# Attention layer, then triangle layer: the second head pair's q and k loaded last in the passage and scored later, the last projections staged in small tiles, token scores and values issued in turn

## The chip, the cores and the metric

The kernel runs on one core of a Trainium2 chip. It is one program for four batch items, without a loop in the instructions: 58551 instructions in a fixed order on each engine. The metric is device time in microseconds. Three runs of the kernel before took 3699.86, 3704.49 and 3706.74 us, so the median is 3704.49 us. Engines are named as in the profile: PE (TensorE matmuls), PEld (its weight loads), DVE (VectorE), ACT (ScalarE), POOL (GpSimd), SP (SyncE, which here only issues DMAs).

## The reference, cut to what matters

Layer 0 is self-attention over 4096 tokens of 256 channels (32 for queries and keys, 128 for values). Layer 1 reads the result as a 64 x 64 grid and runs a triangle attention with 8 heads of 32 channels, an output product, layer norms and an MLP.

```python
def layer0(x):                       # b, 4096, 256
    f, g, v = x @ Wf + bf, x @ Wg + bg, x @ Wh + bh
    beta = softmax(einsum('bqd,bkd->bqk', g, f))
    return x + einsum('bqk,bkd->bqd', beta, v) @ Wo + bo

def layer1(x):                       # b, 64, 64, 256
    q, k, v1, v2 = x @ Wq, x @ Wk, x @ Wv1, x @ Wv2        # 8 heads of 32
    att = softmax(einsum('bilhd,bljhd->biljh', q, k) / sqrt(32), axis=2)
    out = einsum('biljh,bilhd,bljhd->bijhd', att, v1, v2)
    h = layer_norm(x + out @ Wo1)
    return layer_norm(relu(h @ W1 + b1) @ W2 + b2 + h)
```

## The kernel before

The four batch items b = 0 to 3 are handled one after the other. For each, `layer0` computes the token attention and writes the projections q, k, v1, v2 of its result to DRAM; then the triangle stage reads them back, for two heads (a "pair") at a time.

**Token attention.** There are 8 query blocks (`qb`) of 512 tokens and, for each, 8 groups (`k`) of four key tiles; a group is numbered `g`. `scores(g)` (line 526) issues four matmuls s (L531, operands in fp32r) into two PSUM tiles of tag "a" and then two exponentials on ACT (L541), each over half of the tile `e[g]`. `values(g)` (line 544) issues four matmuls o (L552, fp32, which the profile shows as eight passes) and one DVE addition to `esum` (L559). The loop issues `scores(g + 1)` and then `values(g)`, so that the exponentials of g + 1 run beside the values of g. Behind each group a "part" for the block before follows: the normalisation `norm` (L573 den, L575 reciprocal, L577), the output `y` (L598), and the projections (L613, L645). After the eighth group of a block DVE sums `esum` further (L562 to L566), and `norm` waits for that.

**The passage.** Lines 731 to 801 lead from token attention to the triangle stage: `norm(last)`, the last output and its projections, and the first pair's triangle scores (`score(0)` to `score(3)`, L857). Their results are staged in three `stage` tiles, which have the tag "R" of which there are three buffers, and stored on the ACT or SP queue. The products of the triangle stage use the same three buffers. In the passage of b > 0 the token-wise work of the item before (`rest.heads`, `rest.load`, `hidden`) is mixed in. `L.fetch_qk(1)` (line 790) issues the load of the second pair's q and k on the SP queue: four DMAs of 64 rows. Their two buffers are those of the first pair, so the load waits for `score(3)`.

**The triangle stage.** It has 32 steps of 8 rows i. The order of every engine's work is written out by hand in two lists of words, `ORDER0` for b = 0 (a period is four steps) and `ORDER` for b > 0 (a period is two steps). A word is an action, a piece and, behind the slash, by how many periods it lags. The words that matter here:

- `Rxm`: the product of attention and v2 (L959), on POOL for the last two or three m of a step and on DVE for the rest; `Axm`: its accumulation on PE (L969) into PSUM tiles of tag "a", of which there are two; `Txn`: ACT copies one of them out (L979).
- `Wx`, `tx`, `cx`, `Vx`: weights on ACT (L894), their transpose on PE (L911), POOL's copy (L919), the stationary operand (L938).
- `sp`: the triangle scores of the later pairs, one quarter of a pair at a time (L857, PSUM tag "a" too); `e0`, `e1`: their two exponentials (L867). The first `sp` of the stage scores quarter 0 of pair 1. It stands near the front of the first period that has work; pair 1 is first used in step 8.
- `h`, `ht`, `m`, `r`, `z`, `so`, `fo`, `fa`, `pp` and others: the token-wise work of the item before (b > 0), here L1028, L1128, L1161, L1181 on PE and small operations on the other engines. For b = 0, `P`, `C`, `g`, `a`, `b` prepare the inputs of the later items, from a tile `xin` that `ahead.load` fills, and `m`, `n`, `o`, `p` make late projections.

All engines take their instructions in the order in which they are issued. A DMA is issued on the SP queue in its turn, too; an instruction there that has to wait holds up those behind it.

Of the kernel before, what the change touches and what calls it, by code (L numbers as in the profile page):

```python
# [10 lines left out]
F32 = mybir.dt.float32  # L11
# [29 lines left out]


ORDER = """
    r0/1 A10/2 A11/2 m1/1 R14/2 R05/1 S1/1 R15/2 T10/2 sp/1 A14/2 A16/2 r1/1 e0/1 e1/1 A15/2 A05/1 T11/2
    R04/1 A04/1 z0/1 W1/1 R03/1 V1/1 fi/2 S0 z1/1 t1/1 so/1 R06/1 R00/1 c1/1 sa A03/1 R07/1 R02/1 A06/1
    A02/1 A00/1 rr/1 pp/1 W0 R01/1 A07/1 A01/1 fo/1 fa T01/1 R12/1 t0 T00/1 R17/1 h1/-1 R13/1 h0/-1 ht
    R16/1 hU A13/1 hT A12/1 A17/1 R11/1 c0 R10/1 m0 V0
""".split()


# [5 lines left out]
    A21/2 g1/2 S3/1 W1/1 A27/2 A23/2 A26/2 a1/2 V3/2 A24/2 P31/2 C21/2 R32/2 b1/2 m1/2 T20/2 c3/2 P30/2 C31/2  # L56
    t0/1 v2/2 n1/2 R25/2 A25/2 R33/2 sp0/1 T21/2 A32/2 C30/2 R34/2 R36/2 R30/2 A33/2 e00/1 u2/2 e01/1 o1/2 R31/2
    g2/2 P00/1 c0/1 R37/2 A34/2 A36/2 A30/2 A31/2 A37/2 V0/1 R35/2 C00/1 T30/2 t1/1 R00/1 p1/2 P01/1 a2/2 b2/2
    C01/1 A35/2 R03/1 T31/2 A00/1 R02/1 g0/1 a0/1 b0/1 R05/1 R07/1 A05/1 A03/1 v3/2 R06/1 u3/2 m0/1 S2/1 W2/1
    c1/1 v0/1 V1/1 R01/1 A02/1 n0/1 R04/1 A07/1 A01/1 A04/1 R12/1 P11/1 u0/1 P10/1 A06/1 T00/1 sp1/1 C11/1 T01/1  # L60
    R13/1 R15/1 R14/1 A13/1 e10/1 e11/1 t2/1 C10/1 R10/1 A12/1 R17/1 V2/1 A15/1 A14/1 A10/1 R16/1 R11/1 S0 R22/1
    W3/1 g3/2 c2/1 W0 A17/1 R27/1 A11/1 v1/1 R20/1 a3/2 b3/2 u1/1 o0/1 p0/1 S1 R21/1 T10/1 P20/1 t3/1 P21/1
    A16/1 T11/1 C20/1 A20/1 R23/1 A22/1 R24/1 R26/1
""".split()


# [1 line left out]
def attention_then_triangle_kernel(  # L68
# [408 lines left out]
                self.fetched = self.stored  # L477


    def layer0(b, F, safe, rest):  # L480
        yT, gT, fT = F.yT, F.gT, F.fT


# [39 lines left out]
        e, o_ps, esum, oT, ends, parts_of = {}, {}, {}, {}, {}, {}  # L523


        def scores(g):
            qb, k = divmod(g, 8)
            tt, n = divmod(k, 4)
            s_ps = [pa("s") for _ in range(2)]
            for r in range(4):  # L530
                nc.tensor.matmul(  # L531
                    s_ps[r // 2][:, r % 2, :], fT[tt][:, ts(r * 4 + n, P)], gT[qb // 4][:, ts(qb % 4, QB)],
                    start=True, stop=not safe,
                )
                if safe:
                    nc.tensor.matmul(
                        s_ps[r // 2][:, r % 2, :], ones_b[0:1, :], row[qb][0:1, :], start=False, stop=True
                    )
            e[g] = work.tile([P, 4, QB], F32, tag="k8", name="e")
            for j in range(2):  # L540
                nc.scalar.activation(e[g][:, 2 * j : 2 * j + 2, :], s_ps[j], AF.Exp)  # L541


        def values(g):
            qb, k = divmod(g, 8)
            tt, n = divmod(k, 4)
            if k == 0:
                o_ps[qb] = pc("o")
                esum[qb] = work.tile([P, 4, QB], F32, tag="Rp", name="esum")
            es = e.pop(g)  # L550
            for r in range(4):
                nc.tensor.matmul(  # L552
                    o_ps[qb], F.v[tt][:, r * 4 + n, :], es[:, r, :],
                    start=(k == 0 and r == 0), stop=(k == 7 and r == 3),
                )
            if k == 0:
                nc.vector.tensor_copy(esum[qb], es)
            else:
                nc.vector.tensor_tensor(esum[qb], esum[qb], es, ALU.add)  # L559
            if k == 7:  # L560
                halves = esum[qb]
                nc.vector.tensor_tensor(halves[:, 0:2], halves[:, 0:2], halves[:, 2:4], ALU.add)  # L562
                part = parts_of[qb] = work.tile([P, 2, QB], PART, tag="hid", name="part", bufs=1)
                nc.vector.tensor_tensor(part[:, 0], halves[:, 0], halves[:, 1], ALU.add)
                nc.vector.tensor_tensor(halves[:, 2], halves[:, 0], halves[:, 1], ALU.add)
                nc.vector.tensor_tensor(part[:, 1], halves[:, 2], part[:, 0].bitcast(F32), ALU.subtract)  # L566
# [132 lines left out]
            parts[6] = [lambda qb: proj(qb, "q", 1)]  # L699
            parts[7] = [lambda qb: proj(qb, "k", 1)]  # L700
        last = NQB - 1
        scores(0)
        for g in range(8 * NQB):
            qb, k = divmod(g, 8)
            if b == 0 and not safe:
                for load in later[3 * g : 3 * g + 3]:
                    load()
                if g == 6:
                    fold_bias()
                if g == 20:  # L710
                    add_b2()
            if safe and k == 0 and qb + 1 < NQB:
                mx, todo = pieces(qb + 1)
                for qc, t in todo:
                    max_piece(qc, t, mx)
                row[qb + 1] = max_row(mx)
            if g + 1 < 8 * NQB:
                scores(g + 1)
            values(g)

            if qb > 0 and not (qb == last and k >= 6 + late):
                for part in parts[k]:
                    part(qb - 1)
            if qb == last and k == 3:
                L.fetch_v1(0)
                L.fetch_v1(1)
            if qb == last and k == 5:
                if b > 0:
                    rest.load(NP * (b - 1))
                L.fetch_qk(0, True)  # L730
# [4 lines left out]
        old, t0 = b > 0, NP * (b - 1)  # L735
        stage = [work.tile([P, 4, QB], F32, tag="R", name="stage", bufs=3) for _ in range(3)]
        norm(last)
        if old:
            for n in range(2):
                rest.heads(t0, n, psum=pc)  # L740
# [45 lines left out]
        score(3)  # L786
        proj(last, "q", 1, None, stage[1][:, 3, :], nc.scalar)
        L.sums(0)
        proj(last, "k", 1, None, stage[2][:, 0, :], nc.scalar)
        L.fetch_qk(1)  # L790
        L.weights(0)
        hidden(1)
        L.turn(0)
        L.stationary(0)
        if not late:
            proj(last, "v2", 1, None, stage[2][:, 1, :], nc.scalar)
        if old:
            for n in range(2):
                rest.heads(t0 + 1, n)
            rest.load(t0 + 2)  # L800
        return L


# [3 lines left out]
    class Layer1:  # L807
# [10 lines left out]
        def fetch_qk(self, pair, first=False):  # L818
            io, rows = self.io, ts(pair, 64)
            qk = self.qk[pair] = [big.tile([P, 2048], F32, tag="qk", name=name, bufs=2) for name in ("q", "k")]  # L820
            n = 56 if first else 64
            for lh in range(2):
                half, lk = slice(64 * lh, 64 * lh + 64), min(n - 32 * lh, 32) * N
                nc.sync.dma_start(
                    out=qk[0][half, 0 : 32 * n], in_=io["q"][rows, lh, 0:n, :].rearrange("c i l -> c (i l)")
                )
                nc.sync.dma_start(out=qk[1][half, 0:lk], in_=io["k"][rows, 2048 * lh : 2048 * lh + lk])


        def fetch_v2(self, pair, part=None):  # L830
# [510 lines left out]

    def first_layer1(L, ahead, F):
        turned = {}
        ahead.load(0)

        def fetched(step):
            if 24 <= step < 31:
# [28 lines left out]
        for period in range(NSTEP // 4 + 3):  # L1376
            for word, late in words_of(ORDER0):
                i, last = period - late, int(word[-1])
                if word[0:2] == "sp":
                    if i >= 0:  # L1380
                        scores(2 * i + last)
                elif word[0] == "e":
                    if i >= 0:
                        take_scores(2 * i + int(word[1]), last)
                elif word[0] in "RATSWVtc":
                    step_word(word[0], 4 * i + int(word[1]), last)
                elif word[0] in "mnop":
                    if 0 <= i < 4:
                        own.word(word[0], 2 * i + last)
                elif 0 <= i < 4 and int(word[1]) < 2:  # L1390
                    front_word(word[0], 2 * i + int(word[1]), last)
                elif 4 <= i < 8:
                    front_word(word[0], 4 * i - 8 + int(word[1]), last)
# [3 lines left out]
    def next_layer1(b, L, rest, ahead, F):  # L1397
# [90 lines left out]
        for period in range(NP + 4):  # L1488
            for word, late in words_of(ORDER):
                i = period - late  # L1490
                if word[0] in "RATSWVtc":
                    step_word(word[0], 2 * i + int(word[1]), int(word[-1]))
                elif word == "sp":
                    scores(i)
                elif word in ("e0", "e1"):
                    take_scores(i, int(word[1]))
                else:
                    of_piece(word, i)
        assert not held
# [3 lines left out]
    def run(safe):  # L1503
        rest, ahead = Tokens(), Ahead()
        with tc.manual_schedule():
            F = front0(0)
            for b in range(NB):
                L = layer0(b, F, safe, rest)
                F = Front() if b + 1 < NB else None
                if F is None:  # L1510

                    rest.ios.append(L.io)
                if b == 0:
                    first_layer1(L, ahead, F)
                else:
                    next_layer1(b, L, rest, ahead, F)
                if F is not None:
                    rest.ios.append(L.io)
# [51 lines left out]
```

## Time and profile before

The profiled execution took 3700.29 us, of which 3698.4 us lie between its first and last instruction; the rest, 1.9 us, lies around it. The granted TensorE clock was 0.99 on average.

| engine | busy us | share of the span |
|---|---|---|
| PE | 3566.0 | 96% |
| DVE | 2682.0 | 73% |
| ACT | 1918.8 | 52% |
| POOL | 1761.5 | 48% |

The share of the chain that ended last belongs to PE with 80%, to POOL with 9%, to DMA with 3%, to DVE with 3% and to "issue" with 3%. Within the chain the largest lines are o (L552) with 23% and acc (L969) with 17%; s (L531) has 6%, and the transfer `k<-k` 2%.

How to read it: PE's idle time is small on the whole, but not evenly spread. A busy share of 96% says that most stages are bound by PE; where the chain leaves PE for a transfer or another engine, PE stood still. Such places are short and few, so views by time (the chain in order of time, the timeline, the windows) tell more here than sums over the span. A matmul's busy time includes the overlap with its neighbours; the distance between the starts of neighbours is what it costs. The profile shows an fp32 matmul as two passes.

### The profile page before, as it was taken

What the parts mean: (1) busy time and instruction counts of PE and PEld (TensorE: products, weight loads), DVE (VectorE), ACT (ScalarE), POOL (GpSimd) and SP (SyncE); (2) the same over time, 40 slices, a digit from 0 to 9 for tenths busy, and PEclk for the clock granted to TensorE, in tenths of its full rate; (3) what the DMA queues carried; (4) which work ended last, traced back from release to release, by engine and by line L of the source; (5) the groups of instructions that cost most, each with busy time, mean ns of one, the idle gap of its engine ahead of it and who ended that gap; (6) DMA issues with size and microseconds to landing.
All of it is one profiled execution on the core that took longest, in us unless ns stands there. A gap on an engine that the chain in (4) does not pass through costs nothing.

```text
span 3698.4 us, 58551 instructions
## 1 busy us (share of the span) xinstructions
PE 3566.0 (96%) x22602; PEld 1929.6 (52%) x22602; DVE 2682.0 (73%) x2142; ACT 1918.8 (52%) x4257; POOL 1761.5 (48%) x918
## 2 busy tenths in 40 slices
PE   9999899989999999998999999999899999999998
PEld 6555444444555555554455555554355555555477
DVE  4555599897555479999555449999755455999976
ACT  3333465554333367665433347676533335677654
POOL 5000199894000069999100019999700005999920
PEclk9999999999999999999999999999999999999999
DMA  8111566575111344425311153333511125431221
GB/s 149 47 46 46 146 166 161 146 168 147 51 51 52 104 103 94 97 48 100 71 52 51 49 143 89 75 91 65 117 42 50 52 73 136 98 90 49 68 65 56
DMA packets 461232, 324.01 MB, mean 88 GB/s; under 512 B 299984, under 2 KB 418512, under 8 KB 451600
## 3 DMA queue, kind: packets, MB, share of 16 engines
q1 hardware_dynamic: 411904, 293.21, 29.9%
q0 software_dynamic: 36160, 19.94, 4.8%
q10 hardware_dynamic: 12880, 7.01, 0.7%
q8 instruction: 181, 2.97, 0.3%
q14 instruction: 107, 0.88, 0.1%
HBM read 176.37 MB, written 143.65 MB: 87 GB/s over the span
## 4 chain that ended last, share of the span: by engine, by line
PE 80%; POOL 9%; DMA 3%; DVE 3%; issue 3%; ACT 1%; SPq 1%; ACTq 0%; POOLq 0%; DVEq 0%
PE o L552 23%; PE acc L969 17%; PE proj L613 8%; POOL Rp L959 7%; PE s L531 6%; PE mp L1161 5%; PE zp L1181 5%; PE sp L857 3%; PE hp L1028 2%; PE v1p L645 2%; PE y L598 2%; DMA k<-k 2%; DVE R L959 2%; PE att L911 1%; PE v1p L415 1%
## 5 line engine op out<-in xcount | busy, mean ns | idle before, releaser
L959 POOL TENSOR_TENSOR Rp<-attP,v 128x2048 f32<-128x2048 f32 x328 | 1491.2, 4573 | 430.3 <-ACT attP L919 349.5
L959 DVE TENSOR_TENSOR R<-att,v 128x2048 f32<-128x2048 f32 x696 | 1548.7, 2273 | 113.4 <-PE acc L969 71.2
L552 PE MATMUL o<-e,v 128*128 128x512 f32 x2048 | 919.8, 592 | 0.0
L559 DVE TENSOR_TENSOR esum<-esum,e 128x2048 f32<-128x2048 f32 x224 | 512.8, 2289 | 486.0 <-ACT e L541 482.9
L969 PE MATMUL acc<-R,wsel 128*32 128x512 f32 x5568 | 701.3, 601 | 14.9 <-ACT ao L979 7.8
L541 ACT ACTIVATE e<-s 128x1024 f32<-128x1024 f32 x512 | 496.6, 1025 | 312.5 <-PE s L531 152.3
L552 PEld LDWEIGHTS o<-e,v 128*128 128x128 f32 x2048 | 387.5, 189 | 391.8 <-issue 369.9
L1089 POOL TENSOR_SCALAR nt<-mv 128x4 f32<-128x4 f32 (+1 forms) x51 | 9.9, 194 | 1210.1 <-DVE mv L1045 1196.7
L531 PE MATMUL s<-gT,fT 128*128 128x512 f32 x1024 | 362.0, 474 | 8.7 <-ACT e L541 5.5
L969 PE MATMUL acc<-Rp,wsel 128*32 128x512 f32 x2624 | 347.5, 601 | 20.4 <-POOL Rp L959 19.5
L979 ACT COPY ao<-acc 128x1024 f32<-128x1024 f32 x256 | 254.6, 1020 | 177.5 <-PE acc L969 159.4
L969 PEld LDWEIGHTS acc<-R,wsel 128*32 128x32 f32 x5568 | 155.0, 110 | 355.1 <-issue 280.2
L894 ACT ACTIVATE es<-S,rd 128x64 f32<-128x64 f32 x1024 | 257.8, 336 | 15.9 <-DVE rd L886 14.4
L531 PEld LDWEIGHTS s<-gT,fT 128*128 128x128 f32 x1024 | 190.9, 189 | 134.5 <-issue 94.6
L1161 PE MATMUL mp<-hT,w 128*128 128x256 f32 x1024 | 249.5, 389 | 0.7 <-ACT hT L1133 0.7
L575 DVE RECIPROCAL rec<-den 128x512 f32<-128x512 f32 x32 | 107.4, 3358 | 193.4 <-PE den L573 193.4
L1181 PE MATMUL zp<-w,hid 128*128 128x256 f32 x1024 | 245.3, 385 | 0.8 <-ACT hid L1170 0.8
L1161 PEld LDWEIGHTS mp<-hT,w 128*128 128x128 f32 x1024 | 186.5, 190 | 101.4 <-ACT hid L1170 36.9
L1181 PEld LDWEIGHTS zp<-w,hid 128*128 128x128 f32 x1024 | 185.8, 190 | 65.0 <-issue 29.3
L625 ACT COPY st<-proj 128x512 f32<-128x512 f32 x98 | 57.5, 587 | 304.7 <-PE proj L613 169.8
L969 PEld LDWEIGHTS acc<-Rp,wsel 128*32 128x32 f32 x2624 | 80.7, 110 | 202.1 <-issue 125.7
L867 ACT ACTIVATE S<-sp 128x512 f32<-128x512 f32 x128 | 129.8, 1117 | 97.6 <-PE sp L857 74.1
(179 smaller groups left out, 3641.7 us busy)
## 6 DMA issues: line engine op xcount, KB each, us to landing
v<-v2d SPq DMA_DIRECT2D x44, 512.0 KB
v1c<-v1d SPq DMA_DIRECT2D x128, 128.0 KB
aT<-ao SPq DMA_DIRECT2D x1024, 16.0 KB
A<-aT SPq DMA_DIRECT2D x256, 64.0 KB
out_dram<-z SPq DMA_DIRECT2D x63, 256.0 KB
y<-yT SPq DMA_DIRECT2D x56, 256.0 KB
q<-st SPq DMA_DIRECT2D x56, 256.0 KB
k<-k SPq DMA_DIRECT2D x28, 512.0 KB
```

What stands on the lines that cost most here:

```text
L531: nc.tensor.matmul(s_ps[r // 2][:, r % 2, :], fT[tt][:, ts(r * 4 + n, P)], gT[qb // 4][:, ts(qb % 4, QB)], start=True, stop=not safe,)
L541: nc.scalar.activation(e[g][:, 2 * j : 2 * j + 2, :], s_ps[j], AF.Exp)
L552: nc.tensor.matmul(o_ps[qb], F.v[tt][:, r * 4 + n, :], es[:, r, :], start=(k == 0 and r == 0), stop=(k == 7 and r == 3),)
L559: nc.vector.tensor_tensor(esum[qb], esum[qb], es, ALU.add)
L613: nc.tensor.matmul(ps, w[:, cc, rows], y(qb, cc), start=(cc == 0), stop=(cc == 1))
L867: nc.scalar.activation(self.S[pair][:, :, l0 : l0 + 8].rearrange("p i l -> p l i"), sp[:, lh], AF.Copy if self.safe else AF.Exp,)
L894: nc.scalar.mul(e[:, i, :], rows[:, i, :], rec[:, i : i + 1])
L959: eng.tensor_tensor(R, src.unsqueeze(1).to_broadcast([P, D, N]), v2[h], ALU.mult)
L969: nc.tensor.matmul(acc[32 * c : 32 * c + 32, n % 2, :], w[:, n, c, 16 * h : 16 * h + 32], R[:, ts(c, 8), :].rearrange("p d j -> p (d j)"), ...
L979: nc.scalar.copy(self.ao[step][:, ts(np, 2)].rearrange("p k d j -> p k (d j)"), self.acc[step][np])
L1161: nc.tensor.matmul(self.mp[:, fc % 2, :], w1_sb[:, cc, ts(fc, P)], self.hT[tt][:, cc, :], start=(cc == 0), stop=(cc == 1),)
L1181: nc.tensor.matmul(zp[:, n, :], self.hid[tt][:, fc, ts(n, P)], w2_sb[:, fc, :], start=(fc == 0), stop=(fc == 3 and tt not in self.hT2),)
```

## The change

It has four pieces.

1. **Where pair 1's q and k are loaded.** `L.fetch_qk(1)` moves from the middle of the passage to its end, behind the load of the next token tile `rest.load(t0 + 2)`. For pair 1 the load of k is cut in two by columns, so that columns 0 to 511 of both halves come before the rest: two DMAs for q and four for k instead of two and two.
2. **Where pair 1 is first scored.** In both lists new words `sf`, `f0`, `f1` do the first quarter of pair 1; `sp`, `e0`, `e1` skip it. In `ORDER`, `sf` stands at the end of step 0, behind `T01`, `t0` and `T00`; in `ORDER0` it stands directly before `A00`.
3. **Where the last projections are staged.** k and (for b > 0) v2 of the last block use the small tiles of tag "st" instead of `stage[2]`. `stage[2]` then only holds the last block's y. For b = 0, `ahead.load(0)` is issued in the passage, behind `norm(last)`, instead of at the start of the triangle stage.
4. **Token scores and values.** `scores` becomes `score(g, r)`, one matmul; the exponential of a half follows its second matmul. `values(g)` now issues `score(g + 1, r)` before each of its four o matmuls, so the order on PE is s, o, s, o, s, o, s, o instead of s, s, s, s, o, o, o, o.

The arithmetic stays as it was.

```diff
@@ ORDER
-    R04/1 ... A01/1 fo/1 fa T01/1 R12/1 t0 T00/1 R17/1 h1/-1 R13/1 h0/-1 ht
-    R16/1 hU A13/1 hT A12/1 A17/1 R11/1 c0 R10/1 m0 V0
+    ... fo/1 fa T01/1 R12/1 t0 T00/1 sf/1 R17/1 h1/-1 R13/1 f0/1 h0/-1 ht f1/1 R16/1
+    hU A13/1 hT A12/1 A17/1 R11/1 c0 R10/1 m0 V0
@@ ORDER0
-    C01/1 A35/2 R03/1 T31/2 A00/1 R02/1 g0/1 a0/1 b0/1 R05/1 R07/1 ...
+    C01/1 A35/2 R03/1 T31/2 sf0/1 A00/1 R02/1 g0/1 f0/1 a0/1 b0/1 R05/1 f1/1 R07/1 ...
@@ layer0
-        def scores(g):
+        def score(g, r):
...
-            s_ps = [pa("s") for _ in range(2)]
-            for r in range(4):
+            if r == 0:
+                s_of[g] = [pa("s") for _ in range(2)]
+            s_ps = s_of[g]
...
+            if r % 2 == 1:
+                j = r // 2
                 nc.scalar.activation(e[g][:, 2 * j : 2 * j + 2, :], s_ps[j], AF.Exp)
...
             es = e.pop(g)
             for r in range(4):
+                if ahead:
+                    score(g + 1, r)
                 nc.tensor.matmul(
                     o_ps[qb], F.v[tt][:, r * 4 + n, :], es[:, r, :],
...
         norm(last)
+        if late:
+            ahead.load(0)
...
-        proj(last, "k", 1, None, stage[2][:, 0, :], nc.scalar)
-        L.fetch_qk(1)
+        proj(last, "k", 1, None, None, nc.scalar)
         L.weights(0)
...
-            proj(last, "v2", 1, None, stage[2][:, 1, :], nc.scalar)
+            proj(last, "v2", 1, None, None, nc.scalar)
         if old:
             for n in range(2):
                 rest.heads(t0 + 1, n)
             rest.load(t0 + 2)
+        L.fetch_qk(1)
@@ fetch_qk
             for lh in range(2):
-                half, lk = slice(64 * lh, 64 * lh + 64), min(n - 32 * lh, 32) * N
+                half = slice(64 * lh, 64 * lh + 64)
                 nc.sync.dma_start(out=qk[0][half, 0 : 32 * n], in_=...)
-                nc.sync.dma_start(out=qk[1][half, 0:lk], in_=io["k"][rows, 2048 * lh : 2048 * lh + lk])
+            for k0, k1 in ((0, QB), (QB, 2048)) if pair == 1 else ((0, 2048),):
+                for lh in range(2):
+                    half, lk = slice(64 * lh, 64 * lh + 64), min(k1, (n - 32 * lh) * N)
+                    nc.sync.dma_start(out=qk[1][half, k0:lk], in_=...)
@@ first_layer1
-        ahead.load(0)
@@ next_layer1 (first_layer1 alike)
-                elif word == "sp":
-                    scores(i)
-                elif word in ("e0", "e1"):
-                    take_scores(i, int(word[1]))
+                elif word in ("sp", "sf"):
+                    if (i == 0) == (word == "sf"):
+                        scores(i)
+                elif word in ("e0", "e1", "f0", "f1"):
+                    if (i == 0) == (word[0] == "f"):
+                        take_scores(i, int(word[1]))
```

More of the change, by code (lines that the diff above doesn't have):

```diff
@@ L43 @@
 ORDER = """
-    r0/1 A10/2 A11/2 m1/1 R14/2 R05/1 S1/1 R15/2 T10/2 sp/1 A14/2 A16/2 r1/1 e0/1 e1/1 A15/2 A05/1 T11/2
-    R04/1 A04/1 z0/1 W1/1 R03/1 V1/1 fi/2 S0 z1/1 t1/1 so/1 R06/1 R00/1 c1/1 sa A03/1 R07/1 R02/1 A06/1
-    A02/1 A00/1 rr/1 pp/1 W0 R01/1 A07/1 A01/1 fo/1 fa T01/1 R12/1 t0 T00/1 R17/1 h1/-1 R13/1 h0/-1 ht
-    R16/1 hU A13/1 hT A12/1 A17/1 R11/1 c0 R10/1 m0 V0
+    r0/1 A10/2 A11/2 m1/1 R14/2 R05/1 S1/1 R15/2 T10/2 sp/1 A14/2 A16/2 r1/1 e0/1 e1/1 A15/2 A05/1 T11/2 R04/1
+    A04/1 z0/1 W1/1 R03/1 V1/1 fi/2 S0 z1/1 t1/1 so/1 R06/1 R00/1 c1/1 sa A03/1 R07/1 R02/1 A06/1 A02/1 A00/1
+    rr/1 pp/1 W0 R01/1 A07/1 A01/1 fo/1 fa T01/1 R12/1 t0 T00/1 sf/1 R17/1 h1/-1 R13/1 f0/1 h0/-1 ht f1/1 R16/1
+    hU A13/1 hT A12/1 A17/1 R11/1 c0 R10/1 m0 V0
 """.split()
@@ L58 @@
     g2/2 P00/1 c0/1 R37/2 A34/2 A36/2 A30/2 A31/2 A37/2 V0/1 R35/2 C00/1 T30/2 t1/1 R00/1 p1/2 P01/1 a2/2 b2/2
[L59 to L63, printed above, removed]
+    C01/1 A35/2 R03/1 T31/2 sf0/1 A00/1 R02/1 g0/1 f0/1 a0/1 b0/1 R05/1 f1/1 R07/1 A05/1 A03/1 v3/2 R06/1 u3/2
+    m0/1 S2/1 W2/1 c1/1 v0/1 V1/1 R01/1 A02/1 n0/1 R04/1 A07/1 A01/1 A04/1 R12/1 P11/1 u0/1 P10/1 A06/1 T00/1
+    sp1/1 C11/1 T01/1 R13/1 R15/1 R14/1 A13/1 e10/1 e11/1 t2/1 C10/1 R10/1 A12/1 R17/1 V2/1 A15/1 A14/1 A10/1
+    R16/1 R11/1 S0 R22/1 W3/1 g3/2 c2/1 W0 A17/1 R27/1 A11/1 v1/1 R20/1 a3/2 b3/2 u1/1 o0/1 p0/1 S1 R21/1 T10/1
+    P20/1 t3/1 P21/1 A16/1 T11/1 C20/1 A20/1 R23/1 A22/1 R24/1 R26/1
 """.split()
@@ L477, in fetch, with layer0 @@
                 self.fetched = self.stored
-    def layer0(b, F, safe, rest):
+    def layer0(b, F, safe, rest, ahead):
         yT, gT, fT = F.yT, F.gT, F.fT
@@ L523, in layer0, with values @@
         e, o_ps, esum, oT, ends, parts_of = {}, {}, {}, {}, {}, {}
-        def scores(g):
+        s_of = {}
+        def score(g, r):
             qb, k = divmod(g, 8)
             tt, n = divmod(k, 4)
-            s_ps = [pa("s") for _ in range(2)]
-            for r in range(4):
+            if r == 0:
+                s_of[g] = [pa("s") for _ in range(2)]
+            s_ps = s_of[g]
+            nc.tensor.matmul(
+                s_ps[r // 2][:, r % 2, :], fT[tt][:, ts(r * 4 + n, P)], gT[qb // 4][:, ts(qb % 4, QB)],
+                start=True, stop=not safe,
+            )
+            if safe:
                 nc.tensor.matmul(
-                    s_ps[r // 2][:, r % 2, :], fT[tt][:, ts(r * 4 + n, P)], gT[qb // 4][:, ts(qb % 4, QB)],
-                    start=True, stop=not safe,
-                )
[L535 to L540, printed above, removed]
+                    s_ps[r // 2][:, r % 2, :], ones_b[0:1, :], row[qb][0:1, :], start=False, stop=True
+                )
+            if r == 0:
+                e[g] = work.tile([P, 4, QB], F32, tag="k8", name="e")
+            if r % 2 == 1:
+                j = r // 2
                 nc.scalar.activation(e[g][:, 2 * j : 2 * j + 2, :], s_ps[j], AF.Exp)
-        def values(g):
+            if r == 3:
+                s_of.pop(g)
+        def values(g, ahead):
             qb, k = divmod(g, 8)
@@ L701, in layer0 @@
         last = NQB - 1
-        scores(0)
+        for r in range(4):
+            score(0, r)
         for g in range(8 * NQB):
@@ L716, in layer0 @@
                 row[qb + 1] = max_row(mx)
-            if g + 1 < 8 * NQB:
-                scores(g + 1)
-            values(g)
+            values(g, g + 1 < 8 * NQB)
             if qb > 0 and not (qb == last and k >= 6 + late):
@@ L826, in fetch_qk @@
                 )
-                nc.sync.dma_start(out=qk[1][half, 0:lk], in_=io["k"][rows, 2048 * lh : 2048 * lh + lk])
+            for k0, k1 in ((0, QB), (QB, 2048)) if pair == 1 else ((0, 2048),):
+                for lh in range(2):
+                    half, lk = slice(64 * lh, 64 * lh + 64), min(k1, (n - 32 * lh) * N)
+                    nc.sync.dma_start(
+                        out=qk[1][half, k0:lk], in_=io["k"][rows, 2048 * lh + k0 : 2048 * lh + lk]
+                    )
         def fetch_v2(self, pair, part=None):
@@ L1379, in first_layer1 @@
                 if word[0:2] == "sp":
-                    if i >= 0:
+                    if 2 * i + last > 0:
                         scores(2 * i + last)
                 elif word[0] == "e":
-                    if i >= 0:
+                    if 2 * i + int(word[1]) > 0:
                         take_scores(2 * i + int(word[1]), last)
+                elif word[0:2] == "sf":
+                    if i == 0:
+                        scores(0)
+                elif word[0] == "f":
+                    if i == 0:
+                        take_scores(0, last)
                 elif word[0] in "RATSWVtc":
@@ L1507, in run @@
             for b in range(NB):
-                L = layer0(b, F, safe, rest)
+                L = layer0(b, F, safe, rest, ahead)
                 F = Front() if b + 1 < NB else None
```

## The prediction

> **What bounds the kernel.** I first read the chain of waits as a whole: 80% of it is PE, so a stage gains only if PE stands still in it. Then I asked for the chain in order of time. It leaves PE for long in the same place for every item: behind the last projections of the passage. For b = 3, the passage and then the triangle stage:
>
> ```profile
> 3076.61 3.65 PE proj L613 x8
> ...
> 3084.76 10.75 DMA k<-k
> 3095.51 0.14 issue
> 3095.65 2.03 PE sp L857 x62
> 3097.68 3.57 PE acc L969 x16
> 3101.25 2.21 PE zp L1181 x8
> ...
> 3106.06 5.29 PE acc L969 x48
> 3111.34 0.59 PE att L911 x4
> ...
> 3114.53 2.71 PE acc L969 x24
> ```
>
> Columns: start, duration, engine, target, line, count. PE cannot go on before pair 1's q and k have landed. The timeline of PE and DVE says how long each stood still (in brackets: idle before, and what ended it):
>
> ```profile
> 3090.76 0.38 PE L857 MATMUL sp<-q,k 32*64 32x64 f32 x2 [3.21 <-DMA k<-k]
> 3095.65 2.03 PE L857 MATMUL sp<-q,k 32*64 32x64 f32 x62 [4.50 <-DMA k<-k]
> ...
> 3096.21 2.29 DVE L959 TENSOR_TENSOR R<-att,v 128x2048 f32<-128x2048 f32 x1 [6.64 <-DMA v2d<-stage]
> ```
>
> PE idles 7.7 us; DVE waits until 3096.21 for its third buffer R, which is `stage[2]`, held by the v2 store. So two locks open at nearly the same moment, and the change must open both.
>
> The windows add the clock (columns: width, then busy of PE, PEld, DVE, ACT, POOL, then granted clock, DMA share, GB/s):
>
> ```profile
> 3084.00:3102.00 18.00, 10.29 (x99) 5.65 (x98) 9.28 (x10) 5.96 (x19) 11.27 (x3) 0.72 0.79 169
> 3102.00:3120.00 18.00, 18.00 (x134) 9.95 (x135) 14.49 (x7) 12.33 (x39) 13.84 (x11) 1.00 0.07 15
> ```
>
> The clock is 0.72 around the stall and 1.00 behind it. The chain prices this: 16 acc passes take 3.57 us, where 48 take 5.29 later (so 16 cost 1.76). The other passages show the same chain (k<-k of 10.83 us at 1310.54, for instance).
>
> **Pieces 1 to 3, b > 0, worked on b = 3.** *Before:* from the end of the heads at 3087.6 to the next accumulation of step 1 (A13) at 3114.5, 26.9 us. *After*, engine by engine, with the same durations:
>
> - POOL: its two products run 3084.3 to 3093.3 as now, the third follows directly, 4.5 us, to 3097.9. The `pp` polish, 2.0 us (3107.6 to 3109.8 before), ends at 3100.0.
> - DVE: two products and a sum to 3089.5, then, since `stage[2]` is free once the projections have read y (3085.4), R00 to 3091.8, statistics 1.2 to 3093.0, R02 to 3095.3, R01 (whose buffer A03 frees) to 3098.5.
> - PE: A05 waits for POOL's first product until 3088.9, so 1.3 us idle stay. Then A05 and A04 1.8, z 4.1, att 0.4, six accumulations 5.3, att 0.6: 3101.1. None waits; the nearest are A07, 0.8 us behind POOL, and A01, 1.1 us behind R01.
> - ACT: es(1) and the operand of step 1 no longer wait behind the exponentials and are ready by 3089. Behind z come the squares 1.9, copy, roots, es(2) 2.0 (3099.5), then from 3100.0 `fo` and `fa` 1.9, then T01 1.0: 3102.8.
> - `sf` needs a PSUM tile, and the oldest is the one that T01 frees. PE waits 1.7 us here, a **new wait** in front of heads (2.2), htp (0.4) and A13: sf 3102.85 to 3104.8, A13 at 3107.4.
>
> Gain: 3114.5 - 3107.4 = **7.1 us**. With the wait at `sf` gone it would be 8.8; that is the upper end.
>
> Queues. SP: the load of `rest.load(t0 + 2)` waits until 3087.4 for the heads, as now, but no longer behind the lane that the v2 store held (its second DMA went out at 3096.1). Its five issues take 2 us, then the six of q and k follow from about 3089.5 to 3093.3, then v1c. What `sf` needs is both halves of q and 512 columns of k, 1.25 MB. At the 169 to 182 GB/s of these windows that is 7 us plus 1 to 2 for the tile loads ahead: landed near 3098.5, 4 us before `sf`. All 2 MB land near 3103; v1c(2) behind them is needed at about 3109 by V0. Nothing waits, with 4 us to spare. The v2 store, which took from 3086.0 to 3096.1 beside these loads, is ahead of them now.
>
> [...] the change makes six of at most 512 KB out of four. The row: each of these issues takes 0.45 to 0.59 us on SP, so two more cost 1.2 us there, inside the 4 us. [...] by the row it is unchanged as long as `sf` waits for T01. I take the row.
>
> [...] By the idle row alone a passage would gain 7.7 - 1.3 - 1.7 = 4.7 us; with the slow passes (1.8 acc, 0.5 z, 0.1 sp) it is the 7.1 above. The window's 0.72 decides for the latter.
>
> **b = 0.** PE idles 0.9 and 4.5 us before the same scores. Here `sf` comes earlier, at 443.8 (the transposes of xin, 0.7, first; es(1); two more), and the load still starts at 432.25 when `score(3)` ends; its first 1.25 MB should be there near 441.5. But A05 needs the PSUM tile that `f1` frees, and `f1` stands behind `a0`, which needs `g0`: 449.2, where it ran at 451.5. DVE's second product still waits for the q store in `stage[1]` (445.6). PE and DVE both come out **2.4 us** ahead (ends: 0 and 4.2).
>
> **Piece 4, where it loses.** ACT now gets its second half only behind s, o, s, o, s, o, s. The rows that price it, last groups of b = 3:
>
> ```profile
> 3040.55 1.93 ACT L541 ACTIVATE e<-s 128x1024 f32<-128x1024 f32 x2
> ...
> 3042.51 2.29 DVE L559 TENSOR_TENSOR esum<-esum,e 128x2048 f32<-128x2048 f32 x1 [5.52 <-ACT e L541]
> ...
> 3048.17 0.50 PE L573 MATMUL den<-part,ones_f 128*128 128x512 f32 x1 [0.18 <-DVE part L566]
> ```
>
> DVE waits for ACT, PE's den for DVE: no slack for b > 0. The group's s starts at 3039.8. Now both exponentials end 2.7 us later. After: four s at 0.234 and three o at 0.858 make 3.5, plus 0.2 to ACT and 1.03: 4.7. So the den, and everything behind it, is **2.1 us late** for each b > 0. For b = 0 a projection stands between (den at 409.2, DVE done at 407.8), so 0.7.
>
> **Piece 4, inside the 256 groups.** PE's timeline for a group with a projection on each side:
>
> ```profile
> 2863.70 1.88 PE L613 MATMUL proj<-yT,wq 128*128 128x512 f32 x4
> 2865.01 1.50 PE L531 MATMUL s<-gT,fT 128*128 128x512 f32 x4
> 2866.35 3.60 PE L552 MATMUL o<-e,v 128*128 128x512 f32 x8
> 2869.78 0.59 PE L613 MATMUL proj<-yT,wk 128*128 128x512 f32 x1
> ```
>
> o: 3.43 / 8 = 0.429 a pass. The projection's four passes end at 2865.41, so four s take 0.94, 0.234 each, and the last s before o is as long as the others. PE is gapless, so there is no wait to hide; each s, o and its weight load remain. I take 0. [...] The high end is a price per change between fp32r and fp32: 6 more changes in a group, 1536 in all; the rows show under 3 ns (4.6 us). At each start of token attention the first o need not wait for the second scores: 0.2 us (b > 0), 0.8 (b = 0).
>
> **Sum.** b > 0: 3 x (7.1 - 2.1 + 0.2) = 15.6. b = 0: 2.4 - 0.7 + 0.8 = 2.5. Together 18 us: the span 3698.4 becomes 3680, the profiled execution 3700.3 becomes 3682. That execution lay 4.2 us under the median of the three runs, which it shares as an offset, so I predict 3704.5 - 18 = **3686.5 us**.
>
> **Rivals.**
>
> - *R0, as above*: 3680 to 3694. Chance 0.62.
> - *R1, s becomes faster between o's*: [...] Against: the last s, in front of o, is not shorter than the rest now. 0.1.
> - *R2, the gain is swallowed*: `sf` waits for q and k after all, or the den wait (2.1 us idle, in two parts) brings half the clock again. If `sf` had to wait another 4 us in each item, 3704.5 - 18 + 16 = 3702; half of that, 3694. For: between 1755 and 1760 PE is idle for 2.9 of 5 us, and the window 1760.3 to 1763.8 has a clock of 0.51. Against: 4 us to spare. 0.18.
> - *R3, slower*: alternating fp32r and fp32 costs PE at each change. Break-even at 18 / 1536 = 12 ns; at 25 ns, +38 - 18 = +20, 3725. Against: the start of o behind s and of s behind a projection shows nothing of it. 0.05.
> - *R4, the change doesn't do what it says*: o(g, 0) waits for both exponentials. In groups without a part the second ends 4.7 us after the group's start and o(g, 0) stands at 4.6, so 0.2 to 0.4 us in 39 groups: 8 to 16 us, some 3699. Against: the first two `sp` matmuls ran when only their half of q and k had landed, so waits are by region. 0.05.
>
> 0.2% is 7.4 us, about what a measurement can tell from no change: between 3697.1 and 3711.9 is "the same". Faster: R0, R1, half of R2, some of R4: 0.85. Same: the rest of R2 and R4: 0.1. Slower 0.05. Range **3670 to 3698**.
>
> **What would show it.** No idle of PE before `sp` by `k<-k` in any passage; clock 1.00 there; the third R right behind the sum; a wait of 1 to 2 us at `sf` ended by ACT's `ao`; PE's idle before den grown from 0.2 to 2.3 us for b > 0. Starts of s and o 0.234 and 0.429 apart, a group of 4.37. Wrong if the distance of s moves by more than 5 ns, if `sf` is released by a DMA, or if half clock follows the den.

## The result, and the profile after

The changed kernel takes **3686.80 us** (median of 6 runs, 3684.63 to 3689.25), the kernel before 3703.47 us in the 6 runs beside it. The ratio is 0.9954, with an interval of 0.9942 to 0.9967: 16.7 us less. In the profiled executions the span went from 3698.4 to 3683.3 us, 15.1 less, and the mean granted clock from 0.990 to 0.994.

First the chain of waits in order of time, the passage of b = 3 (start, duration, engine, target, line, count):

```profile
3073.95 4.55 POOL Rp L974
3078.51 0.04 issue
3078.55 1.92 PE acc L984 x16
...
3089.58 1.02 ACT z L1120 x2
3090.61 0.91 ACT h L1120 x2
3091.52 0.91 ACT ao L994
3092.43 0.04 issue
3092.47 2.08 PE sp L872 x58
3094.55 1.72 PE hp L1043 x4
...
3099.03 2.71 PE acc L984 x24
```

The 10.75 us of `k<-k` are gone from the chain. In their place stand ACT's two operations `fo` and `fa` (z, h) and the copy `ao` that frees a PSUM tile; then comes `sf`, in the place of the former `sp`. The timeline of PE and DVE at the same place (in brackets: idle before, and what ended it):

```profile
3078.31 0.68 DVE L899 TENSOR_REDUCE dens<-S 128x8 f32<-128x512 f32 x1
3079.02 0.20 DVE L901 RECIPROCAL rd<-dens 128x8 f32<-128x8 f32 x1
3079.14 2.25 DVE L974 TENSOR_TENSOR R<-att,v 128x2048 f32<-128x2048 f32 x1
...
3092.47 2.08 PE L872 MATMUL sp<-q,k 32*64 32x64 f32 x64 [1.59 <-ACT ao L994]
```

DVE's third R follows the sum without a wait; it waited 6.64 us before. PE waits 1.59 us for `ao`, and no longer for a transfer. The windows (width, busy of PE, PEld, DVE, ACT and POOL, clock, DMA share, GB/s):

```profile
3074.00:3092.00 18.00, 15.54 (x107) 8.31 (x105) 16.48 (x13) 11.00 (x41) 17.43 (x11) 1.00 0.80 175
3092.00:3110.00 18.00, 17.53 (x208) 11.28 (x212) 12.59 (x8) 9.57 (x19) 13.63 (x5) 0.91 0.53 123
```

The first shows full clock where 0.72 stood before. The second has 0.91: behind the wait at `sf`, the clock is 0.50 for 3.4 us, from 3094.8 to 3098.2.

Where the time went is best seen by cutting each item at two points: from its first s to its last den (token attention), from there to the first accumulation of step 1 (passage), and from there to its last accumulation (triangle stage). All numbers are differences of starts in the trace, in us; of three numbers, they are b = 1, 2, 3.

| kernel | token attention, b > 0 | passage, b > 0 | triangle, b > 0 | b = 0: all three |
|---|---|---|---|---|
| before | 390.7 391.9 391.9 | 66.0 66.2 66.3 | 428.7 428.6 424.6 | 368.4 55.3 415.1 |
| changed | 392.2 392.5 392.5 | 59.5 59.5 61.1 | 428.5 428.6 424.6 | 369.1 55.1 414.1 |
| changed, again | 392.1 392.4 392.3 | 60.6 59.4 59.4 | 428.3 428.4 424.5 | 370.4 55.6 417.6 |
| group 63 plain | 390.2 390.4 390.5 | 61.0 61.1 61.1 | 428.4 428.5 424.6 | 368.4 55.3 414.7 |
| turns only | 392.2 392.4 392.4 | 65.3 65.3 63.3 | 429.0 428.9 424.6 | 368.6 55.5 415.3 |
| `sf` behind heads | 392.1 392.4 392.4 | 58.7 58.7 58.7 | 428.9 428.9 425.2 | 368.1 53.8 416.8 |
| score later only | 390.4 391.8 391.8 | 65.6 64.1 63.7 | 428.5 428.6 424.6 | 370.0 60.4 416.3 |
| no turns | 390.4 391.9 391.8 | 60.9 60.4 59.4 | 428.3 428.3 424.5 | 369.2 55.3 414.3 |
| load early | 392.2 392.4 392.4 | 60.6 59.4 61.1 | 428.3 428.4 424.5 | 370.4 55.8 417.7 |
| `stage[2]` | 392.2 392.4 392.4 | 62.1 60.6 59.4 | 428.3 428.3 424.5 | 368.8 55.1 414.1 |
| k whole | 392.3 392.5 392.4 | 60.6 59.5 59.5 | 428.5 428.6 424.6 | 369.1 55.6 415.8 |
| three edits | 390.1 390.3 390.4 | 57.6 57.5 57.5 | 428.9 429.0 425.1 | 368.6 53.4 416.8 |
| three edits, again | 390.1 390.3 390.3 | 57.6 57.6 57.5 | 428.9 429.0 425.1 | 367.5 52.0 412.5 |
| three edits, no turns | 390.9 391.8 391.8 | 57.6 57.5 57.5 | 429.0 429.2 425.3 | 370.2 53.3 416.0 |

Two readings. For b > 0 the changed kernel gains 18.4 us in the passages (6.5 + 6.7 + 5.2) and gives back 2.7 in token attention. And b = 0 moves by up to 5 us between two executions of one kernel (its triangle stage took 414.1 and 417.6), so small effects have to be read at b > 0. There two executions of one kernel agree to 0.2 us in each stage, except for steps of 1.1 to 1.7 us in the passage. These steps are half clock, taken up last.

### The profile page after: what moved, and what is told of

It is laid out like the page before. It is cut to its first block, busy times and chain, and to the rows that moved or that the text cites. A ratio compares the mean times of both kernels' runs of the same rounds, so it can differ in the third digit from the quotient of the medians.

```text
span 3683.3 us, 58564 instructions
## 1 busy us (share of the span) xinstructions
PE 3562.0 (97%) x22602; PEld 1930.0 (52%) x22602; DVE 2682.3 (73%) x2142; ACT 1963.3 (53%) x4257; POOL 1763.0 (48%) x918
## 4 chain that ended last, share of the span: by engine, by line
PE 70%; POOL 7%; issue 3%; DMA 3%; DVE 3%; ACT 2%; SPq 0%; ACTq 0%; POOLq 0%; DVEq 0%
PE acc L984 18%; PE o L561 18%; POOL Rp L974 6%; PE proj L622 6%; PE zp L1196 5%; PE mp L1176 5%; PE s L534 5%; PE hp L1043 3%; PE sp L872 3%; PE v1p L654 2%; DVE R L974 1%; PE y L607 1%; PE att L926 1%; PE hp L1048 1%; PE htp L1143 1%
## 5 line engine op out<-in xcount | busy, mean ns | idle before, releaser
L974 POOL TENSOR_TENSOR Rp<-attP,v 128x2048 f32<-128x2048 f32 x328 | 1491.8, 4576 | 420.0 <-ACT attP L934 370.2
L561 PE MATMUL o<-e,v 128*128 128x512 f32 x2048 | 1043.4, 592 | 0.0
L546 ACT ACTIVATE e<-s 128x1024 f32<-128x1024 f32 x512 | 524.0, 1025 | 581.5 <-PE s L534 481.9
L534 PE MATMUL s<-gT,fT 128*128 128x512 f32 x1024 | 785.5, 769 | 8.9 <-ACT e L546 5.1
L1185 ACT ACTIVATE hid<-mp,b_sb 128x256 f32<-128x256 f32 x256 | 105.6, 471 | 117.5 <-PE mp L1176 117.5
```

The costliest lines, as they stand in the source:

```text
L534: nc.tensor.matmul(s_ps[r // 2][:, r % 2, :], fT[tt][:, ts(r * 4 + n, P)], gT[qb // 4][:, ts(qb % 4, QB)], start=True, stop=not safe,)
L561: nc.tensor.matmul(o_ps[qb], F.v[tt][:, r * 4 + n, :], es[:, r, :], start=(k == 0 and r == 0), stop=(k == 7 and r == 3),)
L974: eng.tensor_tensor(R, src.unsqueeze(1).to_broadcast([P, D, N]), v2[h], ALU.mult)
```

## The experiments

**1. Group 63 without turns.** All else as in the changed kernel.

```diff
-                if ahead:
+                if ahead and g + 1 < 8 * NQB - 1:
                     score(g + 1, r)
...
+            if g + 1 == 8 * NQB - 1:
+                for r in range(4):
+                    score(g + 1, r)
             values(g, g + 1 < 8 * NQB)
```

> The changed kernel, but the scores of the last group of each item (g = 63) are issued before the values of group 62, as before the change; all other groups stay in turns. Theory: PE's wait before den (1.23 + 0.77 us for b > 0, 0.52 for b = 0) is only the late second exponential of group 63, so it falls back to 0.2 and 0, and with it the slow output of b = 0 (3.50 us for y, where it took 1.96): 3 x 2.1 + 0.7 + 1.5 = 8 us less than the changed kernel, about 3679. Rival: the lateness is made up behind the den in any case (the passage waits for transfers), or PE's order inside the groups causes it: within 2 us of the changed kernel, about 3687.

Measured: 3680.96 us, ratio 0.9944 (0.9930 to 0.9957). PE's timeline at den for b = 1, changed kernel:

```profile
1274.55 0.47 PE L582 MATMUL den<-part,ones_f 128*128 128x512 f32 x1 [1.23 <-DVE part L573]
1275.79 0.50 PE L582 MATMUL den<-part,ones_f 128*128 128x512 f32 x1 [0.77 <-DVE part L575]
```

and with group 63 plain:

```profile
1272.98 0.50 PE L582 MATMUL den<-part,ones_f 128*128 128x512 f32 x1 [0.18 <-DVE part L575]
```

The two waits of 1.23 and 0.77 us shrink to the 0.18 of the kernel before; token attention falls from 392.2 to 390.2 in b = 1 and by 2.1 and 2.0 in the others. So the late den costs 2.0 to 2.1 us per item. The passages took 61.0 to 61.1 us, and in this execution all three had half clock behind `sf`; in the changed kernel a passage with it took 61.1 us (b = 3), and the two without it 59.5. Against the expectation, y of b = 0 stayed slow, 3.06 us.

**2. Turns alone.** Piece 4 on the kernel before.

> The kernel before with piece 4 alone (token scores and values in turn); loads, staging and the words for pair 1 as before. Theory: per item b > 0 it loses 2.1 us at den and gains 0.5 in the groups and 0 to 0.9 at the start; b = 0 loses 0.7 and perhaps 1.5 by the clock: together 3 to 5 us slower than the kernel before, about 3707, with half clock behind the transfer of k as before. Rival: the turns bring part of the gain of the change, so that it is 3 us or more faster than before.

Measured: 3701.84 us, ratio 1.0001 (0.9993 to 1.0009), so not the loss that was expected. The den is late (token attention +1.5, +0.5, +0.5 against before), but the passage takes 0.7, 0.9 and 3.0 us less. The wait at `sp` says why. Before, b = 1:

```profile
1316.51 0.38 PE L857 MATMUL sp<-q,k 32*64 32x64 f32 x2 [3.17 <-DMA k<-k]
1321.50 2.03 PE L857 MATMUL sp<-q,k 32*64 32x64 f32 x62 [4.62 <-DMA k<-k]
```

With turns alone:

```profile
1320.86 0.41 PE L870 MATMUL sp<-q,k 32*64 32x64 f32 x2 [4.19 <-DMA k<-k]
1323.19 2.04 PE L870 MATMUL sp<-q,k 32*64 32x64 f32 x62 [1.92 <-DMA k<-k]
```

The y of b = 1 was 3.4 us late in this run (1282.05 against 1278.61), and these scores are 1.7 us late: PE waited 6.1 us here instead of 7.8. A lateness ahead of such a wait is in part absorbed by it. In the changed kernel this cover is gone, which is why the 2.1 us count there (experiment 1). The passages of b = 1 and 2 also hold half clock behind the den, 1.2 us each, and that of b = 3 does not.

**3. `sf` behind the heads.** The changed kernel with `sf`, `f0` and `f1` moved back in `ORDER`.

```diff
-    ... T00/1 sf/1 R17/1 h1/-1 R13/1 f0/1 h0/-1 ht f1/1 R16/1 hU A13/1 hT A12/1
+    ... T00/1 R17/1 h1/-1 R13/1 h0/-1 ht sf/1 R16/1 hU A13/1 hT f0/1 f1/1 A12/1
```

> The changed kernel, with sf moved behind h1, h0 and ht in the list for b > 0, and f0, f1 behind hT. Theory: the wait of 1.6 us before sf (ended by ACT's ao) is for the PSUM tile that T01 frees; behind 2.6 us of other PE work the tile is free, so 1.6 us go per item b > 0, and the half clock of 3.4 us behind it in b = 3 (1.6 us more): 5 to 6.5 us less than the changed kernel, about 3681. Rival: sf waits for q and k, or A13 then waits in its place for the second tile that T00 frees: within 1.5 us of the changed kernel.

Measured: 3683.98 us, ratio 0.9949 (0.9935 to 0.9963); the interval overlaps that of the changed kernel. The passages took 58.7 us, although in this execution all three had half clock behind the den (1.2 us each, see the last section). The wait at `sf` therefore costs 1.9 us: 59.4, the best passage of the changed kernel, less 57.5, which is 58.7 less 1.2. The triangle stage gives some of it back: here and in experiment 8 it takes 0.3 to 0.6 us more than in the changed kernel (428.9, 428.9 and 425.2). In the version that combines this with experiment 1, PE's timeline for b = 3 reads:

```profile
3081.12 0.66 PE L929 MATMUL att<-ident,es 128*128 128x128 f32 x4
3081.61 1.07 PE L1046 MATMUL hp<-wo,A 128*128 128x256 f32 x4
...
3083.82 0.60 PE L1146 MATMUL htp<-ident,h 128*128 128x128 f32 x4
3084.35 1.99 PE L875 MATMUL sp<-q,k 32*64 32x64 f32 x64
3086.27 1.92 PE L987 MATMUL acc<-R,wsel 128*32 128x512 f32 x16
```

No line has a bracket: the heads (hp) and htp need no PSUM tile of tag "a", and while they run ACT frees the one that `sf` wants.

**4. The later score alone.** The kernel before with the words `sf`, `f0`, `f1` only: the load early and whole, `stage[2]`, no turns, `ahead.load(0)` where it was.

> The kernel before with piece 2 alone: pair 1 scored at sf, but q and k fetched where they were, k in two DMAs, the last k and v2 staged in stage[2], scores and values not in turns. Theory of two locks: PE is let go, but DVE's third product still waits until the v2 store has landed (the 6.6 us of before), so A02 and A01 wait for DVE; per item b > 0 some 2 to 3 us of the 7 are gained, in all 6 to 10 us less than before, about 3695. Rival: only PE's wait for k counted, and the staging and the order of loads do nothing: 3 x 7 + 2 = 23 us less than before, about 3680.

Measured: 3701.11 us, ratio 0.9996 (0.9987 to 1.0004). This is less than was expected. The passages of b > 0 gain 0.4, 2.1 and 2.6 us, and that of b = 0 loses 5.1, of which 1.4 by a y at half clock (3.31 us instead of 1.96). The timelines of DVE and PE for b = 3, then of PE for b = 0:

```profile
3101.55 2.29 DVE L973 TENSOR_TENSOR R<-att,v 128x2048 f32<-128x2048 f32 x1 [6.52 <-DMA v2d<-stage]
...
3107.16 3.24 PE L983 MATMUL acc<-R,wsel 128*32 128x512 f32 x16 [4.51 <-DVE R L973]
...
450.61 1.08 PE L345 MATMUL tp<-ident,xin 128*128 128x128 f32 x4 [7.64 <-DMA xin<-in_x_dram]
```

With the first lock open (PE no longer waits for k), the second one holds: DVE waits for `stage[2]`, and PE for DVE's R. The v2 store was issued at 3091.5, and DVE was released at 3101.5: 10 us. For b = 0 a third lock appears that the transfer of q and k had covered: the load of `xin`, issued behind them at 438.4. It is the reason for `ahead.load(0)` in the passage; the changed kernel without that one piece was not run.

**5. Which piece opens the second lock.** The changed kernel with the load of pair 1 in its old place ("load early"), and with the last k and v2 in `stage[2]` again.

```diff
-        proj(last, "k", 1, None, None, nc.scalar)
+        proj(last, "k", 1, None, stage[2][:, 0, :], nc.scalar)
...
-            proj(last, "v2", 1, None, None, nc.scalar)
+            proj(last, "v2", 1, None, stage[2][:, 1, :], nc.scalar)
```

> The changed kernel with pair 1's q and k loaded in the old place (directly behind proj k, ahead of the next token tile), the rest of the change kept. Theory (the load can stand anywhere that leaves it 4 us of slack; what counts is that sf is late and the staging small): the q and k land earlier, the token tile 1 to 3 us later but still in time, within 1.5 us of the changed kernel, 3685 to 3688 us. Rival (the 2 MB in front of the token tile delay the heads or the hidden layer, or DVE's y and xc tiles): 2 to 5 us slower in each passage, 3692 to 3700.

> The changed kernel with the last k and v2 staged in stage[2] again, load late. Theory (the third buffer R was locked by the v2 store for 10 us only because q and k were loading beside it; with the load behind, the store is over by the time that DVE wants the buffer, 1 to 3 us later than in the changed kernel at most): 0 to 1 us for each of three items, 3687 to 3690 us. Rival (the small tiles are what opens the lock): DVE's third R 4 us late, A01 and A02 wait 3 to 4 us, and three items lose 3 us each: 3695 to 3697.

Measured: 3684.14 us (ratio 0.9955, 0.9942 to 0.9969) and 3683.92 us (0.9955, 0.9941 to 0.9968), with the kernel before at 3700.89 us beside them. Both ratios are that of the changed kernel. Their best passages, 59.4, are also its best. DVE's timeline with `stage[2]`, b = 3:

```profile
3081.07 0.67 DVE L899 TENSOR_REDUCE dens<-S 128x8 f32<-128x512 f32 x1
3081.78 0.20 DVE L901 RECIPROCAL rd<-dens 128x8 f32<-128x8 f32 x1
3081.90 2.28 DVE L974 TENSOR_TENSOR R<-att,v 128x2048 f32<-128x2048 f32 x1
```

The third R has no bracket: the v2 store, issued at 3078.5, had released the buffer after at most 3.4 us. With q and k loading beside it, it took 10 (experiment 4). So **either** of the two pieces is enough, the store taken from the shared buffer or the load taken from beside the store. With neither (experiment 4) the passages of b > 0 gain 5.1 us in all instead of 18.4. That version also lacks the turns and the split of k, but experiments 6 and 7 take these out one at a time, and the passages of b > 0 stay as short but for half clock. What the score's later place is worth with both pieces kept and `sp` in its old place was not run.

**6. k whole.** The changed kernel with two DMAs for pair 1's k instead of four.

> The changed kernel with k of pair 1 loaded whole (two DMAs of 512 KB) instead of in two parts. Theory (sf waits for T01's PSUM tile, not for the transfer: all 2 MB land about when sf starts): 0 to 1 us per item, sf's wait still ended by ACT's ao: 0 to 3 us above the changed kernel. Rival (the first 512 columns land in time only because they are split off): sf waits 3 to 5 us for k in each of three items, 9 to 15 us slower.

Measured: 3691.09 us (ratio 0.9973, 0.9962 to 0.9984), beside the changed kernel again:

> The changed kernel once more, on the chip of the three runs beside it, so that differences of 2 us can be read: 3686 us, 16 to 18 below the kernel before.

That took 3688.80 us (0.9968, 0.9955 to 0.9980). The intervals overlap. PE's timeline with k whole, b = 3:

```profile
3095.69 2.08 PE L872 MATMUL sp<-q,k 32*64 32x64 f32 x64 [1.61 <-ACT ao L994]
```

`sf` still waits for `ao` and not for k: the split gains nothing that these runs can show.

**7. No turns.** Piece 4 undone in all groups.

> The changed kernel with all scores(g + 1) issued before values(g), as before the change: piece 4 undone in all 256 groups. Theory (the turns gain little in the groups, about 8 ns in each of 256 = 2 us, and lose 2.1 us at each den plus the half clock behind it): like the run with group 63 alone undone, 3681, plus 0 to 2.5: 3681 to 3684 us, so faster than the changed kernel by 3 to 6 us. Groups of 4.355 us against 4.348. Rival (the turns hide something at the start of token attention or give PE more): 3687 or slower.

Measured: 3681.85 us, ratio 0.9951 (0.9938 to 0.9965), 19.0 us below the kernel before where the changed kernel was 16.7 below: the sign as expected, but the two intervals overlap. The table is clearer. Against the changed kernel, token attention of b > 0 is 1.8, 0.6 and 0.7 us shorter without turns. Against group 63 plain it is 0.2, 1.5 and 1.3 us longer. So the turns gain up to 1.5 us in an item and lose 2.1.

The traces show where the gain lies. The start of b = 3, first in the kernel before, then with the turns of the changed kernel:

```profile
2656.30 0.73 PE L531 MATMUL s<-gT,fT 128*128 128x512 f32 x2
...
2659.93 3.60 PE L552 MATMUL o<-e,v 128*128 128x512 f32 x8
```

```profile
2645.36 0.73 PE L534 MATMUL s<-gT,fT 128*128 128x512 f32 x2
2646.40 1.95 ACT L546 ACTIVATE e<-s 128x1024 f32<-128x1024 f32 x2
2647.83 1.02 PE L561 MATMUL o<-e,v 128*128 128x512 f32 x2
```

From the first s to the first o it is 3.63 us before and 2.47 in turns, where three fewer s stand between them (0.70 us), so the start gains 0.46 us. From there to the first o of group 62 both orders issue the same matmuls: 380.8 us without turns and 379.8 with them in b = 2 and 3, but 379.6 and 379.8 in b = 1 (no turns and changed kernel). So the groups gain 1.0 us in two items and lose 0.2 in one. Why is open.

**8. All three.** The changed kernel with experiments 1 and 3, and in `ORDER0` `f1` directly behind `f0`, so that A05 of b = 0 gets its PSUM tile earlier.

```diff
-    ... g0/1 f0/1 a0/1 b0/1 R05/1 f1/1 R07/1 A05/1 ...
+    ... g0/1 f0/1 f1/1 a0/1 b0/1 R05/1 R07/1 A05/1 ...
```

> The changed kernel with three edits: group 63's scores all before values(62), sf behind the heads with f0 and f1 behind hT (b > 0), and for b = 0 f1 directly behind f0. Theory (the den's wait and the wait at sf each cost what the first two runs of them alone showed, and the two add): 5.8 us from the den, 2.8 from sf, about 1 from f1 in b = 0 (A05 waited 1.73 us for f1's tile): 3686.8 - 9.6 = about 3677 us, range 3674 to 3680. PE idle before den 0.2 us in all items, no wait at sf, A05 of b = 0 without its 1.7 us. Rival (each edit only moves the lateness to the next wait, and half clock returns in each passage at another place): 3680 to 3682, no better than the den edit alone.

> The version with group 63 plain, sf behind the heads and f1 directly behind f0, once more: 11 to 13 us below the changed kernel on the same chip.

Measured: 3672.50 us, ratio 0.9923 (0.9910 to 0.9937), below the expected range, and again, on another chip, **3667.35 us**, 0.9909 (0.9893 to 0.9924), beside 3688.80 of the changed kernel there, nearly twice the gain that was expected. At b > 0 the three items take 11.0 us less than in the changed kernel again (by the table, 2626.4 against 2637.4). The rest of the 22.5 us between these two spans lies in b = 0, of which 5.1 in its triangle stage, where nothing differs between the two programs; only the passage's part can be `f1`'s. Its worth shows where y of b = 0 is not at half clock: the passage takes 53.8 us in experiment 3 and 52.0 in the second execution here. The 1.8 us between them is about the 1.73 us that A05 waited for `f1`'s tile there and no longer waits here.

The same with all scores ahead of the values:

> The same version with all scores(g + 1) ahead of values(g), so without turns in any group. Theory (a group in turns is about 8 ns shorter, 2 us in 252 groups, and the first o of each token attention is up to 0.9 us earlier): 2 to 4 us slower than the version with turns in all groups but the last. Rival (turns give nothing, and their only effect is the late den): equal within 1 us.

Measured: 3676.29 us, ratio 0.9927 (0.9913 to 0.9940), 8.9 above. That is more than expected. At b > 0 token attention is 0.8, 1.5 and 1.5 us longer, 3.8 in all, which fits the theory; the rest again lies in b = 0 and was not separated. The turns gain, if the last group of an item has none.

## Why the prediction was right, point by point

The predicted time, 3686.5 us, was met at 3686.8. That it is so close is luck: the gain was 16.7 us and not 18, and the kernel before took 3703.47 us beside these runs, 1.0 less than the 3704.5 from which the sum was taken off. The terms of the sum fared as follows.

- **Passage, 7.1 us each for b > 0: 6.5, 6.7 and 5.2.** The mechanism held in every link: two locks, the order of POOL, DVE and PE behind them, `sf` released by `ao` after 1.6 us (1.7 predicted), a wait of 1.3 us at the first accumulation. The third passage is short by the half clock behind `sf`, 1.6 us, which the sum had not charged.
- **Den 2.1 us late: 2.0 to 2.1** by experiment 1.
- **Groups 0, start 0.2: a gain of 1.0 us in the groups of b = 2 and 3 (a loss of 0.2 in b = 1), and 0.5 at each start**, by experiment 7. The terms were too small; over three items it is a good 3 us.
- **b = 0, a gain of 2.5 us: the first s of b = 1 came 0.3 us later** in the profiled execution (883.6 against 883.3). This step failed. A05 waited for `f1`'s PSUM tile, as the working said, and the den was 0.7 us late. But y ran at half clock, 3.50 us instead of 1.96, so that the passage came out only 0.2 us shorter. The working took the clock of the one profile as a property of the kernel: PE waits 2.55 us for `oT` in front of that y in every version, and half clock followed in 10 of 14 profiles (the longest matmul of y took 1.06 to 1.19 us there, and 0.67 in the other four), not in the kernel before and not in the version of experiment 3. That version, with y at 1.96 us, has a passage of 53.8 us instead of 55.3: even so the gain is 1.5 us and not 2.4. Two other figures vary from one execution to the next: the first s of b = 0 stood at 41.8 us instead of 40.9 (40.9 to 41.8 over all profiles), and the triangle stage of b = 0 took 412.5 to 417.7 us. Late in that stage, between 640 and 883 us, PE is busy for 211 of 243 us before and 212 in the changed kernel, so PE does not bound it; whether a gain of 2 us in the passage would reach its end, no run shows.
- **Six issues for four:** they cost nothing that shows, as the row said. `sf` waited 1.59 us for `ao` with six and 1.61 with four, and going back to two for k gained nothing (experiment 6).
- **Rivals.** R1: s stayed nearly as long as it was; a group (first o to first o, median) takes 6.067 us in turns and 6.080 without, 3 ns less for each s. R2: `sf` never waited for q and k. Its other half, half clock behind the den, did come, in 10 of 21 passages; in the changed kernel behind b = 1 of its second execution (1.2 us). The prediction named this as a sign that it was wrong, and on this point it was: its sum had nothing for half clock. R3: a loss at each change of type was absent, since turns gain. R4: o(g, 0) did not wait for the second half. In experiment 7's rows it starts at 2647.83, when the second exponential still runs (to 2648.35).

So the passages gained 2.9 us less than the sum had it, b = 0 2.8 less, and token attention lost 3.0 less (2.7 instead of 5.7). The last error nearly cancels one of the others; the profiled execution shows 15.1 of the 18 us, the medians 16.7.

## What to carry to other kernels

When a wait for a transfer goes, ask what it covered: here a second lock on a shared buffer (experiment 4), a load queued behind it, and the slack in which a late den cost little (experiment 2). The store that took 10 us beside a load of 2 MB held up nothing once either of the two was moved (experiments 4 and 5). Where scores and values are issued in turn, issue the last group of a chain plain, since its consumer pays for the later exponential (2.0 to 2.1 us an item in experiment 1).

## What the runs showed of the hardware

**Half clock behind the same wait.** Two stretches of the changed kernel around the den of b = 1 (columns as above):

```profile
1272.10:1275.51 3.41, 1.69 (x4) 0.38 (x2) 3.31 (x5) 0.00 (x0) 0.00 (x0) 1.00 1.00 234
1275.51:1278.92 3.41, 3.13 (x15) 2.54 (x16) 2.82 (x2) 0.00 (x0) 0.00 (x0) 1.00 1.03 226
```

and two of the version with `sf` behind the heads, around the same den:

```profile
1272.80:1276.21 3.41, 1.42 (x5) 0.84 (x5) 2.75 (x5) 0.00 (x0) 0.00 (x0) 1.00 1.01 232
1276.21:1279.62 3.41, 3.41 (x11) 2.61 (x11) 3.38 (x2) 0.00 (x0) 0.00 (x0) 0.51 0.99 219
```

The waits, 1.23 and 0.77 us, are the same in both; only in the second does the clock fall behind them, to 0.51. It costs 1.2 us: from den to y it is 4.68 us without and 5.90 with it. So the same wait costs 2.0 us in one run and 3.2 in another. Of the 21 passages with a late den, 10 had it, of the 21 others none. At `sf` it was 8 of 21; the one in the changed kernel (b = 3, clock 0.50) made its passage 1.6 us longer than the other two. What decides whether half clock follows a wait, these runs do not show.

**A store beside a load.** The 256 KB of v2, on the ACT queue, took 10 us beside the 2 MB of q and k in experiment 4 (issued at 3091.5, released at 3101.5), and at most 3.4 us in experiment 5, where q and k were issued only at 3082.3, behind it.
